# Key's product from seven products of halves, with D and value weights kept in DRAM, in an AdaLN layer with a scanned attention and a squared-ReLU mixer

## The chip, the cores and the metric

The kernel runs on one core of one Trainium2 chip. The metric is the device time of one execution in microseconds (us); lower is better. A core has TensorE (PE, the matrix multiplier, with its weight loads listed as PEld), VectorE (DVE), ScalarE (ACT), GpSimd (POOL) and SyncE (SP, which here only issues DMA transfers). Each executes its own instructions in order and waits on semaphores for the others.

## The reference

Inputs are `x` of shape (4, 2048, 512), float32, and weights. Everything is computed in float32.

```python
def layer(x):
    mod = (silu(c) @ wmod).reshape(4, 6, 1, 512)
    sa, ca, ga, sb, cb, gb = (mod[:, i] for i in range(6))
    ga, gb = (sign(g) * max(abs(g), 0.25) for g in (ga, gb))
    h = layernorm(x) * (1 + ca) + sa
    omega, zeta, F = softplus(h @ Wo.T + bo), sigmoid(h @ Wz.T + bz), h @ WB.T + bB
    # a linear recurrence over the 2048 positions, 2 x 64 states, gives xs
    x = x + ga * (xs @ C.T + h @ D.T)
    h = layernorm(x) * (1 + cb) + sb
    prev = shift_by_one_position(h)
    xr, xk = mu_r * h + (1 - mu_r) * prev, mu_k * h + (1 - mu_k) * prev
    k = square(relu(xk @ W_k))           # "Key"
    return x + gb * sigmoid(xr @ W_r) * (k @ W_v)
```

## The kernel before

The 2048 positions are cut into 8 blocks of W = 256, and each block into 4 units, one per batch row, so there are 32 units. Unit i has block s = i // 4 and row b = i % 4 (`at` in the loop). Each unit is worked on by a `Gates` object (its normalisation and the projection for the recurrence) and later by a `Finish` object. The final loop over `fin` runs one unit per turn. In turn i, for i from 4 on, the program order is:

- loads for later units (`load`), issued on SP;
- `key` of unit i (line 516): 16 products of 128x128 weights by 256 columns into two PSUM tiles of the pool tag "pm", which has two buffers. The product of 512 by 512 with 256 positions is cut into four output pieces and four contracted pieces. ACT then applies Relu (521) and Square (522);
- `norm_send(i + 9)`: statistics of a later unit, on ACT and POOL, and their row to DRAM;
- a pull `take(a)` of scan work;
- `attend` of unit i + 1: in two halves, the product with D (line 417, tag "px", three buffers), the product of the scan's states with C (446), then on DVE two additions to x (423, 460) and statistics (122, 123), with a pull `take(a2)` between the halves; then POOL (468, 469) and the normalisation `xn` on ACT (472);
- a pull `take(b_)`;
- `receptance` of unit i (530, tag "pm"), with a sigmoid on ACT (532);
- `mix` of unit i + 1: eight transposes of `xn` on TensorE (491), and from them eight pairs of one ACT (497) and one DVE instruction (500), the four of xk first, then the four of xr; POOL adds the first column (503) and, between the two fours, `shift` adds a row to a later x (410);
- `load_t`, `spread` on SP, and for units that still have a later block, `gates(i + 8)`: a projection (218), its scaling on DVE (224) and four ACT instructions (239);
- `value` of unit i: the product with W_v (545, tag "pm") in two halves, each multiplied and added on DVE (548, 549) and stored by SP (551), with a pull `take(c)` after the first half.

Instructions are issued to each engine in exactly this written order (`manual_schedule`); waits for data and for buffers are added by the framework.

The recurrence of one block (`scan`) is a list of steps, nearly all on DVE, each with a planned cost in us: two `soften` of 3.5, `chunk_step` of 0.7 once and 1.8 seven times, five `join` of 1.0, `fall_start` 0.8, five `fall` of 0.6 and eight `state_step` of 1.25, then `by_batch`, which copies on ACT and sends the states `y` through DMA. `take(budget)` issues steps until their planned costs have used the budget up. A block's scan is begun at the end of the turn with at = 3 (its ACT part, `soften_act`, at once), and pulled in the next three turns. In the turn with at = 2 the four budgets are shares of what is left.

`dg` holds D with the scale and gate of each row b folded in, `wvb` the value weights with the gate of each row folded in. Each is [128, 4, 4, 512] in SBUF, 1 MB per row b, and is built in the first four turns by `Turn` (`turn_d`, `turn_v`). Before, row b is read from place b throughout: `dg[:, u.b, k, :]` (417) and `wvb[:, u.b, k, at]` (545).

Of the kernel before, what the change touches and what calls it, by code (L numbers as in the profile page):

```python
# [21 lines left out]
P = 128  # L22
# [14 lines left out]
class Unit:  # L37


    def __init__(self, i):  # L40
        self.s, self.b = divmod(i, B)
        self.t0 = self.s * W
        self.tag = f"{self.s}_{self.b}"
# [3 lines left out]
def adaln_layer_kernel(ctx: ExitStack, tc: tile.TileContext, x, x_t, c_t, wmod, w_gate, w_b, b_gate, b_f, c_mat, d_mat,  # L47
# [342 lines left out]
    class Finish:  # L390


        def __init__(self, unit):
            self.u, self.tag = unit, f"c{unit.tag}"

        def room(self):
            self.x = p3.tile([P, NT, D], F32, tag="x", name=f"x_{self.u.tag}")

# [13 lines left out]
        def direct(self, n, room=(ps3, "px")):  # L412

            u = self.u
            pd = room[0].tile([P, D], F32, tag=room[1], name=f"pd_{self.tag}_{n}")
            for k in range(KC):
                nc.tensor.matmul(pd, self.h[:, k, ts(n, P)], dg[:, u.b, k, :], start=(k == 0), stop=(k == KC - 1))  # L417
            return pd

        def add_direct(self, n, pd):  # L420
# [4 lines left out]
        def products(self):  # L425

            self.pd = [self.direct(n) for n in range(NT)]
# [48 lines left out]
        def mix(self, between):  # L476
            xn, b = self.xn, self.u.b
            mixed = self.mixed = p1.tile([P, 2, KC, W], F32, tag="mixed", name=f"mixed_{self.tag}")
            edge = p2.tile([P, 2, KC], F32, tag="edge", name=f"edge_{self.tag}")
            if self.u.s == 0:  # L480
                nc.gpsimd.tensor_copy(edge, first_f[:, b])
            else:
                nc.gpsimd.tensor_tensor(
                    edge, prev_f[:, b], carry[:, b, :].unsqueeze(1).broadcast_to([P, 2, KC]), ALU.mult
                )
            pts = []
            for g in range(KC // 2):
                pt = ps2.tile([P, 2, W], F32, tag="pt", name=f"pt_{self.tag}_{g}")
                for j in range(2):
                    for n in range(NT):  # L490
                        nc.tensor.transpose(pt[:, j, ts(n, P)], xn[:, n, ts(2 * g + j, P)], ident)  # L491
                pts.append(pt)

            for i in (1, 0):
                for k in (0, 2, 1, 3):
                    pt, m = pts[k // 2][:, k % 2, :], mixed[:, i, k, :]
                    nc.scalar.activation(  # L497
                        m, pt, AF.Identity, bias=mod[:, SB, k, b : b + 1], scale=now_f[:, b, i, k : k + 1]
                    )
                    nc.vector.scalar_tensor_tensor(  # L500
                        m[:, 1:], pt[:, : W - 1], prev_f[:, b, i, k : k + 1], m[:, 1:], ALU.mult, ALU.add
                    )
                nc.gpsimd.tensor_tensor(mixed[:, i, :, 0], mixed[:, i, :, 0], edge[:, i, :], ALU.add)  # L503
                if i == 1:
                    between()
            for g, pt in enumerate(pts):
                nc.vector.tensor_copy(carry[:, b, 2 * g : 2 * g + 2], pt[:, :, W - 1])

        def key(self):
            mixed = self.mixed  # L510
            act = self.act = p1.tile([P, KC, W], F32, tag="act", name=f"act_{self.tag}")
            for e in range(KC // 2):
                pk = ps2.tile([P, 2, W], F32, tag="pm", name=f"pk_{self.tag}_{e}")
                for j in range(2):
                    for k in range(KC):
                        nc.tensor.matmul(  # L516
                            pk[:, j, :], wk[:, k, ts(2 * e + j, P)], mixed[:, 1, k, :],
                            start=(k == 0), stop=(k == KC - 1),
                        )
                a = act[:, 2 * e : 2 * e + 2, :]  # L520
                nc.scalar.activation(a, pk, AF.Relu)  # L521
                nc.scalar.activation(a, a, AF.Square)

        def receptance(self):
            mixed = self.mixed
# [9 lines left out]
        def value(self, between, parts=1):  # L535

            act, xt, u = self.act, self.x, self.u
            n_col = D // parts
            for n in range(NT):
                pv = ps2.tile([P, D], F32, tag="pm", name=f"pv_{self.tag}_{n}")  # L540
                r = self.r[n]
                for h in range(parts):
                    at = ts(h, n_col)
                    for k in range(KC):
                        nc.tensor.matmul(  # L545
                            pv[:, at], act[:, k, ts(n, P)], wvb[:, u.b, k, at], start=(k == 0), stop=(k == KC - 1)
                        )
                    nc.vector.tensor_mul(r[:, at], pv[:, at], r[:, at])  # L548
                    nc.vector.tensor_add(r[:, at], r[:, at], xt[:, n, at])
                    queue = nc.scalar if h else nc.sync  # L550
                    queue.dma_start(out[u.b, u.t0 + n * P : u.t0 + (n + 1) * P, at], r[:, at])
                if n == 0:
                    between()

    fin = [Finish(Unit(i)) for i in range(NB * B)]
    gts = [Gates(Unit(i)) for i in range(NB * B)]
# [297 lines left out]
    nc.scalar.copy(d0row, pr[:B, :])  # L854
    turn_d[0].turn()
    turn_d[0].keep()
    row = mod_rows(wm_sb, "sb", room=px)
    xt67 = wvb[:, 2].rearrange("p k d -> p (k d)").rearrange("p (i k w) -> p i k w", i=2, k=KC)
    for i in (6, 7):
# [11 lines left out]
    fin[0].products()  # L871
    turn_d[1].turn()
    turn_d[1].keep()
    turn_c[1].rows()
    gts[4].project()
    pcas = [scale_rows(b, pm) for b in range(2, B)]
# [40 lines left out]
    def gates(j):  # L917
        gts[j].project()
        gts[j].multiply()
        gts[j].deliver()  # L920
# [14 lines left out]
    for i, f in enumerate(fin):  # L935
        at = i % B
        ahead = fin[i + 1] if i + 1 < len(fin) else None
        if i < 4:
            if i == 3:
                take(100)  # L940
            fin[i + 2].load()
            gts[i + 10].load()
            f.key()
            if i < 2:
                rows(turn_d[i + 2], turn_c[i + 2])
            if i == 0:
                gts[6].project()
                gts[6].multiply()
                gts[6].deliver(share=True)
            else:  # L950
                norm_send(i + 9)
            if i == 3:
                gates(11)
            take(6)
            ahead.attend(lambda: take(2))
            turn(turn_v[i])
            if i == 0:
                gts[7].project()
                gts[7].multiply()
                gts[7].deliver(share=True)  # L960
                gts[8].norm_dve()
                gts[8].send()
                gts[8].spread()
                gts[9].norm_dve()
                gts[9].send()
            if i == 1:
                gates(9)
            if i:
                take(5)
            f.receptance()  # L970
            ahead.mix(fin[i + 2].shift)
            if i == 0:
                side += scan(1)
                take(0.1)
            gts[i + 9].load_t()
            gts[i + 9].spread()
            if i < 3:
                turn_v[i + 1].rows()
            f.value(lambda: take(3 if i == 0 else 4))
            if i < 2:  # L980
                turn(turn_d[i + 2], turn_c[i + 2])
                gates(8 if i == 0 else 10)
        else:
            if at == B - 1:
                take(100)
            if i + 2 < len(fin):
                fin[i + 2].load()
            if i + 10 < len(gts):
                gts[i + 10].load()
            f.key()  # L990
            if i + 9 < len(gts):
                norm_send(i + 9)
            if at == B - 2:
                left = sum(e[1] for e in side if e)
                a, a2, b_, c = 0.45 * left, 0.11 * left, 0.33 * left, 0.11 * left
            else:
                a, a2, b_, c = 5.5, 1.2, 4.0, 1.2
            take(a)
            if ahead:
                ahead.attend(lambda: take(a2))  # L1000
            take(b_)
            f.receptance()
            if ahead:
                ahead.mix(fin[i + 2].shift if i + 2 < len(fin) else lambda: None)
            if i + 9 < len(gts):
                gts[i + 9].load_t()
                gts[i + 9].spread()
            if i + 8 < len(gts):
                gates(i + 8)
            f.value(lambda: take(c), parts=1 if ahead else 2)  # L1010
        if at == B - 1 and i + 8 < len(gts):
            assert not side
            side += scan(i // B + 2)
            take(0.1)
# [43 lines left out]
```

## Time and profile before

| | before |
|---|---|
| median of 3 runs | 1167.98 us (1167.53 to 1168.3) |
| the profiled execution, own time | 1168.53 us |
| its span in the profile | 1166.8 us |
| granted TensorE clock, mean | 0.993 |
| PE busy | 1146.4 us, 98% |
| DVE busy | 704.1 us, 60% |
| ACT busy | 562.9 us, 48% |
| POOL busy | 160.7 us, 14% |
| moved by DMA | 102.29 MB, mean 88 GB/s |

The profile describes one execution. A row of a group gives the source line, the engine, the operation, output<-inputs, the shape and count, then busy time, mean nanoseconds of one, and the engine's idle time just before, with what ended it. A timeline row gives start and length in us, then the same names, and in brackets the idle time before. A row of a stretch (A:B) gives its length and the busy time with the count of instructions of PE, PEld, DVE, ACT and POOL in this order, then granted clock, DMA share and GB/s. Matmuls are pipelined, so the length of one record is longer than the distance to the next; the distance is what a stream costs.

### The profile page before, as it was taken

Reading aid. Unit: us, or ns where it says so; the run is one execution under the profiler, and the core shown is the slowest. Engines: PE = TensorE matmul, PEld = TensorE weight load, DVE = VectorE, ACT = ScalarE, POOL = GpSimd, SP = SyncE. Lnnn points to the kernel's source line nnn. Section 1 sums busy time; section 2 is a strip of 40 time slices with the busy share of each in tenths; the row PEclk is TensorE's granted clock in tenths of the full one; section 3 lists DMA queues with packets and bytes.
Section 4 is the critical chain, followed back from the end, with each engine's and each line's share of the span. In section 5 each row is a group of like instructions: output and inputs, shape, how many; then the busy total and the mean of one; then the engine's idle time right before and its main releaser. Section 6 shows DMA issues by size and latency. Waiting matters only on the chain.

```text
span 1166.8 us, 12040 instructions
## 1 busy us (share of the span) xinstructions
PE 1146.4 (98%) x3768; PEld 671.9 (58%) x3768; DVE 704.1 (60%) x1919; ACT 562.9 (48%) x1046; POOL 160.7 (14%) x290
## 2 busy tenths in 40 slices
PE   7998999999999999999999999999999999999998
PEld 3454666655655666556566655555666555555555
DVE  5696577548753677537763586537764497633332
ACT  1656777565334653546345644445454533333331
POOL 0132101111101111111111111101111111111100
PEclk9998999999999999999999999999999999999999
DMA  9744353232333322233234322342323111121101
GB/s 316 252 117 83 72 105 90 76 82 80 89 89 102 90 86 86 59 95 96 80 88 113 86 71 65 87 112 78 94 73 83 32 44 55 54 63 55 54 19 37
DMA packets 116801, 102.29 MB, mean 88 GB/s; under 512 B 14721, under 2 KB 87425, under 8 KB 116737
## 3 DMA queue, kind: packets, MB, share of 16 engines
q1 hardware_dynamic: 113728, 100.20, 30.8%
q0 software_dynamic: 320, 0.53, 0.3%
q10 hardware_dynamic: 2688, 0.79, 0.3%
q8 instruction: 30, 0.49, 0.2%
q14 instruction: 35, 0.28, 0.1%
HBM read 80.49 MB, written 16.81 MB: 83 GB/s over the span
## 4 chain that ended last, share of the span: by engine, by line
PE 96%; DVE 2%; ACT 1%; DMA 0%; issue 0%; POOL 0%; SPq 0%; DVEq 0%
PE pk_c L516 19%; PE pv_c L545 19%; PE pr_c L530 19%; PE pd_c L417 18%; PE pg L218 9%; PE pc_c L446 5%; PE pt_c L491 2%; PE turn_d L720 1%; PE turn_v L720 1%; PE rows_ca L633 1%; PE pd L118 0%; PE pca L118 0%; DMA wvb<-in_wmod_dram 0%; PE rows_sb L633 0%; PE rows_mean L633 0%; PE rows_gb L633 0%
## 5 line engine op out<-in xcount | busy, mean ns | idle before, releaser
L516 PE MATMUL pk_c<-mixed_c,wk 128*128 128x256 f32 x1024 | 229.4, 383 | 4.6 <-POOL mixed_c L503 4.6
L417 PE MATMUL pd_c<-dg,xt 128*128 128x512 f32 x512 | 231.7, 596 | 0.0
L545 PE MATMUL pv_c<-wvb,act_c 128*128 128x512 f32 (+1 forms) x528 | 225.5, 580 | 1.1 <-DVE r_c L548 1.1
L530 PE MATMUL pr_c<-wr,mixed_c 128*128 128x512 f32 x512 | 224.9, 592 | 0.0
L516 PEld LDWEIGHTS pk_c<-mixed_c,wk 128*128 128x128 f32 x1024 | 196.6, 192 | 44.5 <-issue 13.9
L500 DVE SCALAR_TENSOR_TENSOR mixed_c<-pt_c,prev_f,mixed_c 128x255 f32<-128x255 f32 x256 | 118.1, 482 | 131.4 <-ACT mixed_c L497 131.4
L472 ACT ACTIVATE xn_c<-x,nmr_c,rstd_c 128x512 f32<-128x512 f32 x64 | 48.6, 806 | 257.7 <-POOL nmr_c L469 257.7
L530 PEld LDWEIGHTS pr_c<-wr,mixed_c 128*128 128x128 f32 x512 | 97.1, 190 | 120.2 <-issue 119.6
L417 PEld LDWEIGHTS pd_c<-dg,xt 128*128 128x128 f32 x512 | 97.8, 191 | 111.0 <-issue 108.0
L545 PEld LDWEIGHTS pv_c<-wvb,act_c 128*128 128x128 f32 x528 | 99.3, 190 | 107.9 <-issue 102.6
L423 DVE SCALAR_TENSOR_TENSOR x<-pd_c,rs,x 128x512 f32<-128x512 f32 x64 | 47.7, 747 | 156.2 <-PE pd_c L417 156.2
L497 ACT ACTIVATE mixed_c<-pt_c,mod,now_f 128x256 f32<-128x256 f32 x256 | 130.4, 561 | 11.6 <-DVE mixed_c L500 5.3
L521 ACT ACTIVATE act_c<-pk_c 128x512 f32<-128x512 f32 x64 | 38.2, 598 | 187.9 <-PE pk_c L516 187.9
L218 PE MATMUL pg<-xt,wgb 128*128 128x256 f32 x448 | 103.0, 384 | 0.0
L548 DVE TENSOR_TENSOR r_c<-pv_c,r_c 128x512 f32<-128x512 f32 (+1 forms) x66 | 44.4, 672 | 76.6 <-PE pv_c L545 74.0
L218 PEld LDWEIGHTS pg<-xt,wgb 128*128 128x128 f32 x448 | 84.2, 193 | 10.7
L410 POOL TENSOR_TENSOR x<-x,d 128x1024 f32<-128x1024 f32 x31 | 73.0, 2355 | 0.8 <-ACT d L757 0.8
L446 PE MATMUL pc_c<-cg,y 128*128 128x512 f32 x128 | 65.1, 593 | 1.3 <-DMA y<-pre 1.3
L239 ACT ACTIVATE pre<-g,bias 64x256 f32<-64x256 f32 x64 | 46.9, 733 | 38.7 <-DVE g L224 32.3
L468 POOL TENSOR_TENSOR rstd_c<-rstd_c,neg_half 128x2 f32<-128x2 f32 x32 | 24.4, 762 | 298.1 <-DVE nmr_c L467 298.1
L532 ACT ACTIVATE r_c<-pr_c 128x512 f32<-128x512 f32 x64 | 37.0, 590 | 49.0 <-PE pr_c L530 48.9
L184 POOL TENSOR_SCALAR var<-var 128x2 f32<-128x2 f32 x26 | 5.1, 197 | 378.5 <-ACT xs L180 378.4
(189 smaller groups left out, 1108.0 us busy)
## 6 DMA issues: line engine op xcount, KB each, us to landing
xt<-in_x_t_dram SPq DMA_DIRECT2D x116, 256.0 KB, 5.3
x<-in_x_dram SPq DMA_DIRECT2D x32, 512.0 KB, 3.9
out_dram<-r_c SPq DMA_DIRECT2D x62, 256.0 KB, 2.1
xs<-in_x_dram SPq DMA_DIRECT2D x54, 256.0 KB, 4.2
wvb<-in_wmod_dram SPq DMA_DIRECT2D x5, 1024.0 KB, 10.2
y<-pre SPq DMA_DIRECT2D x64, 64.0 KB, 2.0
bc<-st SPq DMA_DIRECT2D x24, 128.0 KB, 4.8
wvb<-in_x_t_dram SPq DMA_DIRECT2D x8, 256.0 KB, 10.5
```

What stands on the lines that cost most here:

```text
L218: nc.tensor.matmul(self.pg[:, i, :], wgb[:, b, k, ts(i, P)], self.xt[:, k, :], start=(k == 0), stop=(k == KC - 1))
L239: nc.scalar.activation(there, here, AF.Identity, bias=bias[src, i, b : b + 1])
L410: nc.gpsimd.tensor_tensor(xt, xt, d0[:, self.u.b, :].unsqueeze(1).broadcast_to([P, NT, D]), ALU.add)
L417: nc.tensor.matmul(pd, self.h[:, k, ts(n, P)], dg[:, u.b, k, :], start=(k == 0), stop=(k == KC - 1))
L423: nc.vector.scalar_tensor_tensor(xt, pd, r, xt, ALU.mult, ALU.add)
L446: nc.tensor.matmul(pc, y_of[u.s][:, u.b, ts(n, P)], cg[:, u.b, :], start=(self.row is None), stop=True)
L472: nc.scalar.activation(self.xn[:, n, :], xt[:, n, :], AF.Identity, bias=nmr[:, n : n + 1], scale=rstd[:, n : n + 1])
L497: nc.scalar.activation(m, pt, AF.Identity, bias=mod[:, SB, k, b : b + 1], scale=now_f[:, b, i, k : k + 1])
L500: nc.vector.scalar_tensor_tensor(m[:, 1:], pt[:, : W - 1], prev_f[:, b, i, k : k + 1], m[:, 1:], ALU.mult, ALU.add)
L516: nc.tensor.matmul(pk[:, j, :], wk[:, k, ts(2 * e + j, P)], mixed[:, 1, k, :], start=(k == 0), stop=(k == KC - 1),)
L530: nc.tensor.matmul(pr, mixed[:, 0, k, ts(n, P)], wr[:, k, :], start=(k == 0), stop=(k == KC - 1))
L545: nc.tensor.matmul(pv[:, at], act[:, k, ts(n, P)], wvb[:, u.b, k, at], start=(k == 0), stop=(k == KC - 1))
```

## The change

From unit 4 on (`fast`, block s > 0), Key is computed by a scheme of seven products of halves (Winograd's form of Strassen's). The weight W_k, with 512 contracted by 512 output columns, and the mixed input, with 512 by 256 positions, are each cut into two by two quarters. Seven products of quarters, of 256 by 256 by 128, take the place of the eight that a product by quarters needs.

- `make_key_weights` forms four sums of weight quarters once, with four DVE instructions, in the turn i = 2. They lie in the room of `dg` for row 2.
- `key_sums` forms four sums of input quarters for each unit, on DVE, in `mix` after the four instructions of xk and before `shift`. They lie in the room of `dg` for row 3, in two halves used in turn.
- `key_fast` has four groups of products (two, two, two and one), each group in a tile of tag "pm", 28 matmuls of 128x128 by 128 columns. One copy and seven additions take the products from PSUM to `act`: the additions are on DVE, the copy is on DVE for row b = 0 and on ACT for the others. Relu and Square follow on ACT, now from `act`.
- With two rows of `dg` used for the sums, D of a fast unit is read from place i % 2, and so are its value weights. All four rows of both are stored once to DRAM (`keep_in_dram`, eight DMAs on SP), and for units 6 to 31 both are fetched from there (`fetch`, 1 MB each, on SP): D for unit i + 3 after `attend` of turn i, value weights for unit i + 2 at the end of turn i.
- The budgets of the pulls change: from 5.5, 1.2, 4.0, 1.2 to 3.0, 0, 7.0, 1.2 (at = 0) and 3.6, 1.2, 5.5, 1.2 (at = 1), and for at = 2 the shares from 0.45, 0.11, 0.33, 0.11 to 0.33, 0.11, 0.45, 0.11.

```diff
+            self.fast = unit.s > 0
+            self.at = unit.i % 2 if self.fast else unit.b
...
-                nc.tensor.matmul(pd, self.h[:, k, ts(n, P)], dg[:, u.b, k, :], start=(k == 0), stop=(k == KC - 1))
+                nc.tensor.matmul(pd, self.h[:, k, ts(n, P)], dg[:, self.at, k, :], start=(k == 0), stop=(k == KC - 1))
...
                 if i == 1:
+                    if self.fast:
+                        self.key_sums()
                     between()
...
+        def key_sums(self):
+            (b00, b01), (b10, b11) = self.quarters = [
+                [self.mixed[:, 1, 2 * k : 2 * k + 2, ts(t, P)] for t in range(2)] for k in range(2)
+            ]
+            half = dg[:, 3].rearrange("p k d -> p (k d)")[:, ts(self.u.i % 2, 2 * D)]
+            t = self.sums = half.rearrange("p (i k w) -> p i k w", i=4, k=2)
+            nc.vector.tensor_sub(t[:, 0], b01, b00)
+            nc.vector.tensor_sub(t[:, 1], b11, t[:, 0])
+            nc.vector.tensor_sub(t[:, 2], b11, b01)
+            nc.vector.tensor_sub(t[:, 3], b10, t[:, 1])
+
+        def key_fast(self):
+            (b00, b01), (b10, b11) = self.quarters
+            t, s = self.sums, key_weights
+            act = self.act = p1.tile([P, KC, W], F32, tag="act", name=f"act_{self.tag}")
+            (c00, c01), (c10, c11) = [[act[:, 2 * o : 2 * o + 2, ts(h, P)] for h in range(2)] for o in range(2)]
+
+            def products(*pairs):
+                pk = ps2.tile([P, 2, 2, P], F32, tag="pm", name=f"pk_{self.tag}")
+                for n, (left, right) in enumerate(pairs):
+                    for j in range(2):
+                        for k in range(2):
+                            nc.tensor.matmul(
+                                pk[:, n, j, :], left[:, k, ts(j, P)], right[:, k, :], start=(k == 0), stop=(k == 1)
+                            )
+                return pk[:, 0], pk[:, 1]
+
+            add = nc.vector.tensor_add
+            x1, x2 = products((wk[:, 0:2, : D // 2], b00), (wk[:, 2:4, : D // 2], b10))
+            copy = nc.scalar.copy if self.u.b else nc.vector.tensor_copy
+            copy(c01, x1)
+            add(c00, c01, x2)
+            x6, x5 = products((s[:, 1], t[:, 1]), (s[:, 0], t[:, 0]))
+            add(c10, c01, x6)
+            add(c01, c10, x5)
+            x7, x3 = products((s[:, 2], t[:, 2]), (s[:, 3], b11))
+            add(c11, c01, x7)
+            add(c10, c10, x7)
+            add(c01, c01, x3)
+            x4, _ = products((wk[:, 2:4, D // 2 :], t[:, 3]))
+            add(c10, c10, x4)
+            for e in range(KC // 2):
+                a = self.act[:, 2 * e : 2 * e + 2, :]
+                nc.scalar.activation(a, a, AF.Relu)
+                self.squares(e)
...
-                            pv[:, at], act[:, k, ts(n, P)], wvb[:, u.b, k, at], start=(k == 0), stop=(k == KC - 1)
+                            pv[:, at], act[:, k, ts(n, P)], wvb[:, self.at, k, at], start=(k == 0), stop=(k == KC - 1)
...
+    def make_key_weights():
...
+        nc.vector.tensor_add(s[:, 0], a10, a11)
+        nc.vector.tensor_sub(s[:, 1], s[:, 0], a00)
+        nc.vector.tensor_sub(s[:, 2], a00, a10)
+        nc.vector.tensor_sub(s[:, 3], a01, s[:, 1])
...
+    def keep_in_dram(name, b):
+        src = dg if name == "dg" else wvb
+        nc.sync.dma_start(kept[name][b], src[:, b].rearrange("p k d -> p (k d)"))
+
+    def fetch(name, i):
+
+        if 6 <= i < len(fin):
+            dst = dg if name == "dg" else wvb
+            nc.sync.dma_start(dst[:, i % 2].rearrange("p k d -> p (k d)"), kept[name][i % B])
...
+            if i == 2:
+                make_key_weights()
             ahead.attend(lambda: take(2))
             turn(turn_v[i])
+            keep_in_dram("wv", i)
+            if i == 3:
+                fetch("dg", i + 3)
...
-            f.key()
+            f.key_fast()
...
-                a, a2, b_, c = 0.45 * left, 0.11 * left, 0.33 * left, 0.11 * left
+                a, a2, b_, c = 0.33 * left, 0.11 * left, 0.45 * left, 0.11 * left
             else:
-                a, a2, b_, c = 5.5, 1.2, 4.0, 1.2
+                a, a2, b_, c = (3.6, 1.2, 5.5, 1.2) if at else (3.0, 0.0, 7.0, 1.2)
             take(a)
             if ahead:
                 ahead.attend(lambda: take(a2))
+            fetch("dg", i + 3)
             take(b_)
...
             f.value(lambda: take(c), parts=1 if ahead else 2)
+            fetch("wv", i + 2)
```

More of the change, by code (lines that the diff above doesn't have):

```diff
@@ L40, in __init__ @@
     def __init__(self, i):
+        self.i = i
         self.s, self.b = divmod(i, B)
@@ L507, in mix, with squares @@
                 nc.vector.tensor_copy(carry[:, b, 2 * g : 2 * g + 2], pt[:, :, W - 1])
+        def squares(self, e):
+            a = self.act[:, 2 * e : 2 * e + 2, :]
+            nc.scalar.activation(a, a, AF.Square)
         def key(self):
@@ L519, in key @@
                         )
-                a = act[:, 2 * e : 2 * e + 2, :]
-                nc.scalar.activation(a, pk, AF.Relu)
-                nc.scalar.activation(a, a, AF.Square)
+                nc.scalar.activation(act[:, 2 * e : 2 * e + 2, :], pk, AF.Relu)
+                self.squares(e)
[9 more added lines that the diff above has]
+            nc.vector.tensor_sub(t[:, 3], b10, t[:, 1])
@@ new lines, in key_fast @@
+        def key_fast(self):
[27 more added lines that the diff above has]
+            for e in range(KC // 2):
+                a = self.act[:, 2 * e : 2 * e + 2, :]
+                nc.scalar.activation(a, a, AF.Relu)
+                self.squares(e)
@@ L553, in value @@
                     between()
+    key_weights = dg[:, 2].rearrange("p k d -> p (k d)").rearrange("p (i k o) -> p i k o", i=4, k=2)
+    def make_key_weights():
+        s = key_weights
+        (a00, a01), (a10, a11) = [
+            [wk[:, 2 * k : 2 * k + 2, ts(o, D // 2)] for k in range(2)] for o in range(2)
+        ]
+        nc.vector.tensor_add(s[:, 0], a10, a11)
+        nc.vector.tensor_sub(s[:, 1], s[:, 0], a00)
+        nc.vector.tensor_sub(s[:, 2], a00, a10)
+        nc.vector.tensor_sub(s[:, 3], a01, s[:, 1])
+    kept = {
+        name: [dram.tile([P, KC * D], F32, tag=f"{name}{b}", name=f"{name}{b}") for b in range(B)]
+        for name in ("dg", "wv")
+    }
+    def keep_in_dram(name, b):
[5 more added lines that the diff above has]
+            nc.sync.dma_start(dst[:, i % 2].rearrange("p k d -> p (k d)"), kept[name][i % B])
     fin = [Finish(Unit(i)) for i in range(NB * B)]
@@ L856, in adaln_layer_kernel @@
     turn_d[0].keep()
+    keep_in_dram("dg", 0)
     row = mod_rows(wm_sb, "sb", room=px)
@@ L873, in adaln_layer_kernel @@
     turn_d[1].keep()
+    keep_in_dram("dg", 1)
     turn_c[1].rows()
@@ L981, in adaln_layer_kernel @@
                 turn(turn_d[i + 2], turn_c[i + 2])
+                keep_in_dram("dg", i + 2)
                 gates(8 if i == 0 else 10)
```

## The prediction

> **What bounds the kernel now.** I read the page's busy shares and its chain first, then TensorE's timeline over one unit, then the busy time of every engine unit by unit, then who waits for whom.
>
> ```profile
> PE 1146.4 (98%) x3768; PEld 671.9 (58%) x3768; DVE 704.1 (60%) x1919; ACT 562.9 (48%) x1046; POOL 160.7 (14%) x290
> ...
> PE 96%; DVE 2%; ACT 1%; DMA 0%; issue 0%; POOL 0%; SPq 0%; DVEq 0%
> ```
>
> The end is set by TensorE's own stream. Nothing else is worth shortening, and anything that makes TensorE wait is paid in full. One unit on TensorE, without a gap:
>
> ```profile
> 627.65 7.07 PE L516 MATMUL pk_c<-mixed_c,wk 128*128 128x256 f32 x32
> 634.56 3.60 PE L417 MATMUL pd_c<-dg,xt 128*128 128x512 f32 x8
> ...
> 643.14 7.03 PE L530 MATMUL pr_c<-wr,mixed_c 128*128 128x512 f32 x16
> 650.01 1.04 PE L491 MATMUL pt_c<-ident,xn_c 128*128 128x128 f32 x8
> ...
> 654.34 7.03 PE L545 MATMUL pv_c<-wvb,act_c 128*128 128x512 f32 x16
> 661.20 7.07 PE L516 MATMUL pk_c<-mixed_c,wk 128*128 128x256 f32 x32
> ```
>
> From start to start Key takes 6.91 us: 32 records, 215.9 ns each. The unit takes 33.55 us. The four units of a block (at = 0 to 3), with DVE in the third column of busy times:
>
> ```profile
> 526.99:560.55 33.56, 33.56 (x110) 19.83 (x109) 27.71 (x64) 19.62 (x37) 5.06 (x8) 1.00 0.28 83
> 560.55:594.10 33.55, 33.55 (x110) 19.82 (x108) 23.76 (x79) 14.61 (x28) 4.60 (x8) 1.00 0.31 82
> 594.10:627.65 33.55, 33.55 (x109) 19.83 (x108) 19.42 (x61) 16.38 (x32) 4.72 (x8) 1.00 0.31 83
> 627.65:661.20 33.55, 33.55 (x109) 19.83 (x108) 12.06 (x25) 16.63 (x31) 4.58 (x8) 1.00 0.39 98
> ```
>
> DVE has 12 us of the unit's own work and 7 to 16 us of scan in three of the four. It executes in order, so where its spare time lies decides. The granted clock is 1.00.
>
> **TensorE's part.** A fast unit (4 to 31, so 28 of them) has 28 products of 128x128 by 128 columns. Each fp32 product shows as two records, so 32 records become 56. Their pace is the first unknown. From below: half of 215.9, 108 ns. From above: a load not overlapped at all, 192 ns. The trace has the very form in L209, 128x128 f32 by 128 columns, and a load-bound run in L799 (4 columns):
>
> ```profile
> 35.69 0.36 PE L209 MATMUL pb<-cg,ones 128*128 128x128 f32 x1
> ...
> 35.69 0.69 PE L209 MATMUL pb<-cg,ones 128*128 128x128 f32 x4
> ...
> 33.88 1.86 PEld L799 LDWEIGHTS pbias<-mod,wraw 128*128 128x128 f32 x16 [0.35 <-DVE mod L795]
> ```
>
> These L209 lines are the timeline up to 35.8 us and up to 36.15: three more records end 0.33 us later, 110 ns each. L799's 16 loads take (1.86 - 0.19) / 15 = 111 ns each. I take 111.5: 56 x 111.5 = 6.24 us, a saving of 0.665 us a unit, 18.6 us over 28.
>
> [...] L209's rows are fp32 and of the right width, and the one-pass transposes agree (L491: (1.04 - 0.273) / 7 = 110 ns), so the rows decide. Only four two-pass records in a row have been seen, so a few ns stay open; each costs 1.57 us over 28 units before waits.
>
> **DVE's part.** Added per unit: four sums of quarters in the mix, and one copy and seven adds in Key (from unit b = 1 on, ACT makes the copy). All are 128x256 f32:
>
> ```profile
> L549 DVE TENSOR_TENSOR r_c<-r_c,x 128x256 f32<-128x256 f32 x4 | 1.7, 425 | 0.1
> L548 DVE TENSOR_TENSOR r_c<-pv_c,r_c 128x256 f32<-128x256 f32 x4 | 1.7, 424 | 18.3 <-PE pv_c L545 18.3
> ```
>
> PSUM or SBUF makes no difference. Dependent ones start 0.46 apart (L548 to L549 at 1156.08); independent ones overlap by 0.09 (L299 to L300: 0.36 long, 0.27 apart), so 0.34. Sums: 0.46 + 3 x 0.34 = 1.5 us. Key: about 2.8. Bounds for each of the twelve: 0.3 us if they overlap better (192 elements start 0.27 apart), 0.6 if each exposes a semaphore's delay. They are purely added, so none can gain.
>
> Now the queues, with t = 0 at Key's first record and about 0.2 us from a matmul's slot to its reader (L545 to L548). Product groups occupy TensorE at 0, 1.78, 3.57 and 5.35, to 6.24. DVE first ends the previous unit's value (two of 0.69, from 0.2 to 1.6), then the copy and first add (to 2.8), frees the third group's bank before 3.57, does two adds (3.8 to 4.45, before 5.35), three (5.56 to 6.7) and the last (to 7.0). So Key's own handshakes fit, with 0.7 us to spare each. But DVE is now tied to Key until 7.0, where before it ran 5 to 7 us of scan. That scan moves behind.
>
> - at = 3, no scan: attend and mix are at their old places; the sums lie in idle time (6.1 us before the mix now). Full saving.
> - at = 0: pull 3.0 is one soften (3.7, to 10.7; its ACT part ended at 3.3 before, 4.5 now). Attend's second half waits for TensorE at 14.2 and ends at 16.85. Pull 7.0 is a soften, the first chunk and two more (7.9 with a wait for three ACT copies), to 24.8, so the mix starts 2 us late: four at 0.46, sums 1.5, four at 0.46, carry, gate product, value's first product end at 31.5, its add 32.2, a chunk at 34.0. The next Key starts at 32.9; its second group needs the bank of value's second product, free at 34.75, against 34.67: 0.1 us lost.
> - at = 1: the same path ends with nothing lost.
> - at = 2: 13.0 of planned scan is left (8.75 before, since the first two units pull less). The share of 0.33 pulls five falls and two state steps, 3.5 + 2.3 us, so attend starts at 12.85 (before: DVE waited 4.4 us for TensorE here). Then first half 2.4, two states 2.3, second half 2.65: 20.2. POOL 1.2, ACT's two xn 1.5: 22.9 to 23.0. TensorE finishes receptance at 21.7 and wants xn for the transposes: 1.36 us lost.
> - Units 24 to 27 have no gates, so TensorE has 3.45 us less from transposes to Key, and the same DVE work: 0.4 + 1.1 + 1.4 + 0.9 + 0.2 = 4.0 on top of the 1.36.
> - Last unit: receptance waits for the third group's adds, 0.5.
>
> Lost: 6 x 1.36 + 5 x 0.1 + 4.0 + 0.5 = 13.2 us. The same bookkeeping with before's order gives no wait and 33.56 us a unit.
>
> **What I cost at nothing.** SP gets eight stores and 52 fetches of 1 MB. Each issue is about 0.4 us in a queue that already sits waiting for DVE's results (396.6 us at L551 in SP's waits). The value weights' fetch waits for value's last matmul, but stands behind the output, which is ready 1.4 us later; D's fetch waits for attend at 13.9, with the statistics' row and the next transposed loads behind it, which are wanted a unit later. Each fetch is issued over one unit before its use; 1 MB took 10.2 us. Traffic rises from 83 to about 146 GB/s; the first slice of the page moved 316. The row of y (eight DMAs, 8.8 us from the first ACT copy to landing) is issued ahead of the value fetch and lands at about 8.5, wanted at 9.7. That is the thinnest cover: without it, up to 1 us in each of 6 blocks. POOL's edge (0.2 us) ends before the fourth mix instruction does, so the sums do not wait for it. Key's weight sums (four of 0.69, once) lie in the 3.03 us that DVE idles at 199 to 202. ACT keeps its two Relu and two Square; a Relu from PSUM (0.60) and a Square from SBUF (0.63) last alike, and value wants them 17 us later.
>
> **Sum.** -18.6 + 13.2 = -5.4, against the profiled execution: span 1166.8, own time 1168.5, 0.55 above the median. 1168.0 - 5.5 = 1162.5.
>
> **The rivals.**
> 1. As worked, 0.46: 1162.5, its own range 1158 to 1166.
> 2. Nearly the full saving, 0.14: the scan's real order leaves DVE room. All twelve at 0.34 or less and scan 5% shorter give -12; -18.6 with no wait: 1149 to 1156. For it: at = 3 is idle. Against: the 20.2 at at = 2 is a chain of measured durations.
> 3. Slower, 0.27: DVE's in-order lag. Each added instruction takes 0.6 as it waits for its predecessor's result, and sums 2.2. The mix then ends 0.7 us later in every scan unit and value's banks free late, in the gateless units every time. The same bookkeeping gives +7, and +11 with the scan 3% longer: 1175 to 1179. It decides from about 0.5 us of extra sums per unit. For: the at = 0 unit is full already. Against: the 424 ns rows.
> 4. Slower, 0.08: the two-pass pace does not hold 56 long. Break-even at 115 ns; 120 gives +6, 134 gives +27: 1174 to 1195.
> 5. Late fetches or y, 0.05: 1 us in 28 units gives 1190. This is also the case in which the change doesn't do what it says, its fetched weights not coming beside other work. Against: DMA share 0.31.
>
> About 0.2% (2.3 us) is what a measurement of this kernel can tell. Faster: 0.40 of case 1 and case 2, 0.54. Same: 0.06, 0.05 of case 3 and 0.02 of the rest, 0.13. Slower: 0.33. Range 1153 to 1180: it leaves out the best of case 2 and the worst of 4 and 5.
>
> **What would show it.** Right: 56 records in 6.2 us at Key; the transposes waiting on ACT's xn by about 1.4 us in every third unit of a block; units of 32.9, 33.0, 34.3, 32.9. Wrong: Key's groups waiting on DVE inside Key (case 3), loads spaced over 115 ns (4), TensorE waiting on a DMA into dg, wvb or y (5), no wait at the transposes (2).

## The result, and the profile after

| | before | after |
|---|---|---|
| median of 4 runs each, one chip | 1167.76 us (1166.87 to 1168.3) | 1194.98 us (1194.51 to 1199.47) |
| ratio, 95% interval | | 1.0242 [1.0217, 1.0268] |
| span of the profiled execution | 1166.8 us | 1192.7 us |
| PE busy | 1146.4 us, 98% | 1140.3 us, 96% |
| DVE busy | 704.1 us | 867.1 us |
| moved by DMA | 102.29 MB | 165.32 MB |

The change is slower, by 27.2 us in the medians and 25.9 us in the spans. The forecast was 1162.5 us, with a range up to 1180, so it missed in sign and size. The chain that ended last, from the page of the kernel after:

```profile
PE 65%; DVE 26%; ACT 5%; issue 3%; DMA 1%; POOL 0%; DVEq 0%; SPq 0%; POOLq 0%
```

Before, TensorE was 96% of the chain. Now 26% of it runs over DVE: TensorE's stream has holes, and DVE's order fills them. The products themselves did what was forecast. TensorE's timeline at a Key that waits for nothing (start, length, engine, line, output<-inputs):

```profile
327.16 1.95 PE L562 MATMUL pk_c<-mixed_c,wk 128*128 128x128 f32 x16
328.94 2.84 PE L562 MATMUL pk_c<-dg 128*128 128x128 f32 x24
331.62 1.06 PE L562 MATMUL pk_c<-mixed_c,dg 128*128 128x128 f32 x8
332.51 1.06 PE L562 MATMUL pk_c<-dg,wk 128*128 128x128 f32 x8
333.41 3.60 PE L422 MATMUL pd_c<-dg,xt 128*128 128x512 f32 x8
```

56 records take 6.25 us from start to start (333.41 - 327.16), 111.6 ns each, where Key took 6.91. But the four units of a block, at = 0 to 3 (length, then busy time of PE, PEld, DVE, ACT and POOL, then clock, DMA share and GB/s), do not get shorter:

```profile
531.60:565.10 33.50, 33.03 (x134) 19.81 (x132) 28.30 (x61) 20.52 (x37) 4.82 (x8) 1.00 0.72 146
565.10:599.30 34.20, 33.26 (x133) 20.17 (x134) 30.21 (x81) 15.61 (x32) 5.09 (x8) 1.00 0.69 142
599.30:633.20 33.90, 33.31 (x134) 19.92 (x133) 29.62 (x97) 14.31 (x29) 4.85 (x8) 1.00 0.68 144
633.20:667.40 34.20, 33.16 (x133) 20.07 (x132) 18.09 (x37) 17.32 (x35) 4.63 (x8) 1.00 0.67 158
```

They were 33.55 each; forecast were 32.9, 33.0, 34.3 and 32.9. What TensorE waits for (us in total, times, longest):

```profile
PE pk_c L562 <- DVE r_c L610: 22.6, 18, 3.3
PE pk_c L562 <- DVE act_c L571: 5.4, 5, 1.2
...
PE pt_c L496 <- ACT xn_c L477: 3.7, 12, 0.4
```

Key waits 28.0 us for DVE. L610 is the product by which the *previous* unit's value frees a bank of the tag "pm". None of this was in the list of before. So DVE reaches value's arithmetic late. What makes it late stands in its groups by form (busy us, mean ns of one, idle before):

```profile
L546 DVE TENSOR_TENSOR dg<-mixed_c 128x256 f32<-128x256 f32 x28 | 67.3, 2403 | 0.0
...
L580 DVE TENSOR_TENSOR act_c<-act_c,pk_c 128x256 f32<-128x256 f32 x28 | 11.6, 416 | 0.1
```

The added instructions last 0.41 to 0.43 us each, but for one: the first sum of a unit lasts 2.40 us in the mean. Its two inputs are ready and it shows no idle time before it. The timeline of POOL and DVE around one of them shows what runs beside it:

```profile
285.63 0.20 POOL L508 TENSOR_TENSOR mixed_c<-mixed_c,edge_c 128x4 f32<-128x4 f32 x1 [7.92 <-ACT mixed_c L502]
285.78 2.35 POOL L415 TENSOR_TENSOR x<-x,d 128x1024 f32<-128x1024 f32 x1
...
285.93 2.48 DVE L546 TENSOR_TENSOR dg<-mixed_c 128x256 f32<-128x256 f32 x1
288.44 0.42 DVE L547 TENSOR_TENSOR dg<-mixed_c,dg 128x256 f32<-128x256 f32 x1
```

POOL's `shift` (L415, 2.35 us), issued right behind the edge (L508), starts 0.15 us before the sum, and the sum ends 0.28 us after it: 285.78 + 2.35 = 288.13, against 288.41. The sum looks as if it stood still while `shift` ran. The wait is inside a busy record (2.48 us, with no idle time before it), so no list of waits names it. Only the mean of the group, 2403 ns, betrays it. In the same unit TensorE's next Key then looks so:

```profile
292.98 2.02 PE L562 MATMUL pk_c<-mixed_c,wk 128*128 128x128 f32 x16 [0.47 <-DVE r_c L610]
295.94 2.94 PE L562 MATMUL pk_c<-dg 128*128 128x128 f32 x24 [0.94 <-DVE r_c L610]
```

The theory to be tested (L, the lock): a DVE instruction with two inputs from SBUF does not proceed while `shift` runs on GpSimd, so the first sum waits for the whole of it. The rivals: the seven products with twelve added DVE instructions are too much for DVE wherever the sums stand (D); the 63 MB of added DMA traffic (fetches and stores) disturb the others (F).

### The profile page after: what moved, and what is told of

The parts are those of the page before. It is cut to its first block, busy times and chain, and to the rows that moved or that the text cites. A ratio compares the mean times of both kernels' runs of the same rounds, so it can differ in the third digit from the quotient of the medians.

```text
span 1192.7 us, 13937 instructions
## 1 busy us (share of the span) xinstructions
PE 1140.3 (96%) x4440; PEld 680.1 (57%) x4440; DVE 867.1 (73%) x2238; ACT 567.4 (48%) x1067; POOL 163.4 (14%) x290
## 2 busy tenths in 40 slices
DMA packets 125449, 165.32 MB, mean 139 GB/s; under 512 B 15680, under 2 KB 88384, under 8 KB 117696
## 4 chain that ended last, share of the span: by engine, by line
PE 65%; DVE 26%; ACT 5%; issue 3%; DMA 1%; POOL 0%; DVEq 0%; SPq 0%; POOLq 0%
PE pd_c L422 14%; PE pk_c L562 13%; PE pr_c L592 12%; PE pv_c L607 9%; PE pg L219 6%; PE pc_c L451 4%; DVE dg L546 4%; DVE mixed_c L505 3%; PE pk_c L527 2%; ACT mixed_c L502 2%; DVE stats_c L123 1%; DVE x L465 1%; DVE uv L363 1%; DVE r_c L610 1%; PE pt_c L496 1%
## 5 line engine op out<-in xcount | busy, mean ns | idle before, releaser
L502 ACT ACTIVATE mixed_c<-pt_c,mod,now_f 128x256 f32<-128x256 f32 x256 | 130.4, 561 | 111.5 <-DVE mixed_c L505 107.9
L562 PE MATMUL pk_c<-dg 128*128 128x128 f32 x672 | 83.9, 281 | 10.6 <-DVE act_c L571 5.4
L562 PEld LDWEIGHTS pk_c<-dg 128*128 128x128 f32 x672 | 80.1, 197 | 12.8 <-DVE act_c L571 6.4
L583 ACT ACTIVATE act_c<-act_c 128x512 f32<-128x512 f32 x56 | 34.8, 622 | 109.2 <-DVE act_c L578 109.2
L562 PEld LDWEIGHTS pk_c<-mixed_c,wk 128*128 128x128 f32 x448 | 55.7, 199 | 34.8 <-issue 34.3
L562 PE MATMUL pk_c<-mixed_c,wk 128*128 128x128 f32 x448 | 58.2, 286 | 17.4 <-DVE r_c L610 17.4
L415 POOL TENSOR_TENSOR x<-x,d 128x1024 f32<-128x1024 f32 x31 | 72.8, 2349 | 0.0
L546 DVE TENSOR_TENSOR dg<-mixed_c 128x256 f32<-128x256 f32 x28 | 67.3, 2403 | 0.0
```

What stands on the lines that cost most here:

```text
L415: nc.gpsimd.tensor_tensor(xt, xt, d0[:, self.u.b, :].unsqueeze(1).broadcast_to([P, NT, D]), ALU.add)
L502: nc.scalar.activation(m, pt, AF.Identity, bias=mod[:, SB, k, b : b + 1], scale=now_f[:, b, i, k : k + 1])
L546: nc.vector.tensor_sub(t[:, 0], b01, b00)
L562: nc.tensor.matmul(pk[:, n, j, :], left[:, k, ts(j, P)], right[:, k, :], start=(k == 0), stop=(k == 1))
```

## Experiments

All comparisons are with the kernel before, run on the same chip, where its median is 1166.28 us for the first four experiments and 1167.05 us for the other four. "Units" are distances from one Key's first record to the next.

### The change without `shift`

The fast turns leave out `shift`, so the row that it adds to a later x is missing from the output. The last of the first four turns keeps its own.

```diff
-                ahead.mix(fin[i + 2].shift if i + 2 < len(fin) else lambda: None)
+                ahead.mix(lambda: None)
```

> The changed kernel, but the POOL instruction `shift` behind the first edge of each fast mix is left out (so the row d0 is not added to x there). Lock theory (the first of the four key sums, with two SBUF inputs, stands still while POOL's 2.35 us `shift` runs): the first sum falls from 2.4 us to 0.42 us in all 28 units, TensorE's waits on value's banks at Key's first groups fall from 28 us in total to a few, and the time is about 1163 us (the prediction's working without the stall, 1160 to 1168). Rival A (fetch traffic slows the sums or SP): the first sum stays at 2.4 us, the time stays within 3 us of 1195. Rival B (DVE simply has too many instructions): the first sum gets short, but the time stays above 1180.

Measured: 1163.06 us (1159.28 to 1163.97), ratio 0.9967 [0.9957, 0.9977]. The first sum's group, and TensorE's waits:

```profile
L546 DVE TENSOR_TENSOR dg<-mixed_c 128x256 f32<-128x256 f32 x28 | 13.7, 488 | 0.0
```
```profile
PE pk_c L562 <- DVE r_c L610: 4.9, 5, 1.9
```

27 first sums last 0.42 us and the one that still has its `shift` 2.48; their mean is the 488 ns. Key's waits for value fall from 22.6 to 4.9 us. The units of a block are 32.90, 32.90, 33.90 and 32.90. So with `shift` gone the change gains, and DVE's added work as such does not make it slow: D falls. This kernel also has 59 us less of POOL work (104.0 against 163.4), so it does not yet show that the *meeting* of the two instructions is the cause.

### The sums moved, `shift` kept

The four sums are issued between the halves of value, after its first product and addition, when `shift` is over.

```diff
-                    if self.fast:
-                        self.key_sums()
...
-            f.value(lambda: take(c), parts=1 if ahead else 2)
+            f.value(lambda: (ahead.key_sums() if ahead else None, take(c)), parts=1 if ahead else 2)
```

> The changed kernel with the four key sums issued later on DVE, between the two halves of value instead of between the two fours of the mix; nothing is left out. `shift` then runs beside mix instructions that read PSUM and one SBUF tensor. Lock theory: every sum 0.42 us, time about 1164 us (1160 to 1169; the bookkeeping gives 3.4 us below before). Rival A (traffic): sums elsewhere long again, time near 1195. Rival B (amount of DVE work, which is the same here): time stays above 1180.

Measured: 1162.37 us (1160.68 to 1163.4), ratio 0.9963 [0.9948, 0.9978]. Key waits 3.2 us for value, in two. The timeline of POOL and DVE:

```profile
282.93 2.36 POOL L415 TENSOR_TENSOR x<-x,d 128x1024 f32<-128x1024 f32 x1
...
287.60 0.42 DVE L544 TENSOR_TENSOR dg<-mixed_c 128x256 f32<-128x256 f32 x1
```
Every instruction of the change is there, `shift` included. Only the order differs, and 32.6 us of the 1194.98 are gone (in ratios to before, 0.9963 against 1.0242). It is the meeting, not the work.

### The fetches alone

The kernel before with D and value weights kept in DRAM and fetched as in the change; Key and the budgets as before.

> The kernel before with only the storage part of the change: D and value weights of the later blocks stored to DRAM and fetched for each unit, Key as before, budgets as before. Lock theory: the fetches are not the cause, 1168 us within 2 us. Rival A (traffic or SP's queue): a large part of the 27 us is here, 1180 or more.

Measured: 1166.17 us, ratio 1.0001 [0.9993, 1.001], units 33.55. The fetches cost nothing: F falls.

### One subtraction in the kernel before, from SBUF and from PSUM

If L holds, it needs no Strassen. The kernel before gets one 128x256 subtraction in front of `shift`, in units 4 to 31, into a buffer that is free there. In the first form both inputs lie in SBUF, in the second the first input is the PSUM tile of the transposes.

```diff
                 if i == 1:
+                    if self.u.s:
+                        probe = xn[:, 0, : 2 * P].rearrange("p (k w) -> p k w", k=2)
+                        nc.vector.tensor_sub(probe, mixed[:, 1, 2:4, P:], mixed[:, 1, 0:2, P:])
                     between()
```
```diff
-                        nc.vector.tensor_sub(probe, mixed[:, 1, 2:4, P:], mixed[:, 1, 0:2, P:])
+                        nc.vector.tensor_sub(probe, pts[1][:, :, P:], mixed[:, 1, 0:2, P:])
```

> The kernel before plus one DVE subtraction per unit from block 1 on, 128x256, both inputs in SBUF, at the place of the first key sum; its result is not used. Lock theory: it lasts 2.4 to 2.5 us instead of 0.42 us although there is no fetch and no fast Key here, and the kernel gets slower: with 2.48 us inserted the bookkeeping gives 13 us more, 1178 to 1182, lost in units with at = 0 and in the units without gates. Rival A (fetch traffic makes the sum long): 0.42 us and 1168.

> As the kernel before with one DVE subtraction per unit at the place of the first key sum, but with its first input read from PSUM (the transposed tile) and the second from SBUF; same size, place and wait, result not used. Lock theory (two SBUF inputs are what meets `shift`): 0.42 us each, time 1166 to 1168 as before. Rival C (any DVE instruction issued there is slow, by the wait on POOL's edge or on the queue): 2.3 us each and about 1179 as with two SBUF inputs.

Measured: from SBUF 1178.59 us (1178.13 to 1179.07), ratio 1.0103 [1.0088, 1.0118]; from PSUM 1167.48 us (1166.36 to 1168.17), ratio 0.9998 [0.9989, 1.0006]. The group and the timeline, from SBUF:

```profile
L507 DVE TENSOR_TENSOR xn_c<-mixed_c 128x256 f32<-128x256 f32 x28 | 64.2, 2291 | 1.0
```
```profile
555.27 2.34 POOL L410 TENSOR_TENSOR x<-x,d 128x1024 f32<-128x1024 f32 x1
...
555.55 2.35 DVE L507 TENSOR_TENSOR xn_c<-mixed_c 128x256 f32<-128x256 f32 x1
```

and from PSUM:

```profile
L507 DVE TENSOR_TENSOR xn_c<-pt_c,mixed_c 128x256 f32<-128x256 f32 x28 | 11.6, 415 | 0.0
```
```profile
551.00 2.35 POOL L410 TENSOR_TENSOR x<-x,d 128x1024 f32<-128x1024 f32 x1
...
551.15 0.41 DVE L507 TENSOR_TENSOR xn_c<-pt_c,mixed_c 128x256 f32<-128x256 f32 x1
```

One operation, one size, one place, beside the same 2.35 us of `shift`: 2.29 us or 0.415. Only the first input, and with it the memory that it lies in, separates them. For `shift`, L is shown, and a single such instruction per unit is worth 1% of this kernel. It also accounts for why `mix` itself, in the trace of before, runs beside `shift` at its usual 0.48 us: its instructions (L500, 482 ns in the mean of all 256) take one tensor from PSUM and one from SBUF.

### `shift` in two halves

If the sum waits for one whole GpSimd instruction, two shorter ones might let it in between.

```diff
-            nc.gpsimd.tensor_tensor(xt, xt, d0[:, self.u.b, :].unsqueeze(1).broadcast_to([P, NT, D]), ALU.add)
+            for n in range(NT):
+                nc.gpsimd.tensor_tensor(xt[:, n, :], xt[:, n, :], d0[:, self.u.b, :], ALU.add)
```

> The changed kernel with `shift` as two POOL instructions of 128x512 in place of one of 128x1024. Lock theory, held for one POOL instruction at a time: if DVE gets its turn between the two, the first sum lasts about 1.2 to 1.5 us and the bookkeeping gives 5 us above before, about 1172; if the second half takes the port again at once, the sum stays at 2.4 us and the time at about 1194. A theory in which the two only share bandwidth expects no change in the sum, 2.4 us.

Measured: 1190.69 us (1189.88 to 1191.47), ratio 1.0202 [1.0187, 1.0217]. The timeline:

```profile
287.61 2.67 POOL L416 TENSOR_TENSOR x<-x,d 128x512 f32<-128x512 f32 x2
...
287.76 1.40 DVE L547 TENSOR_TENSOR dg<-mixed_c 128x256 f32<-128x256 f32 x1
289.19 1.37 DVE L548 TENSOR_TENSOR dg<-mixed_c,dg 128x256 f32<-128x256 f32 x1
```

The first sum gets in after the first half (1.40 us), and then the second sum waits for the second half (1.37 us). The turns alternate, one instruction each. The four sums take 3.47 us from the first start to the last end, against 3.60 with one `shift` and 1.54 with none beside them. The two shorter instructions divide the wait here and hardly shorten it. The expectation missed this: it put the time near 1172 if DVE got its turn, and DVE got it, but only for one instruction.

### `shift` at the end of the mix

The order the other way round: the sums stay and `shift` is issued after the second edge of fast units.

```diff
                     if self.fast:
                         self.key_sums()
-                    between()
+                    else:
+                        between()
...
+            if self.fast:
+                between()
```

> The changed kernel with the key sums in their place and POOL's `shift` issued behind the second edge instead of the first; nothing is left out. Lock theory: the sums are all 0.42 us; `shift` now meets carry, the gate product and value's first product (one SBUF input each, not held up) and then value's addition of two SBUF inputs or a scan chunk, which is held up by up to 0.9 us in units with gates and 1.5 us in those without: 1163 to 1172. Rival B (amount of DVE work): above 1180.

Measured: 1167.96 us (1166.95 to 1168.97), ratio 1.0008 [0.9999, 1.0016]. All sums last 0.42 us. The group of value's addition and the timeline of POOL and DVE:

```profile
L614 DVE TENSOR_TENSOR r_c<-r_c,x 128x512 f32<-128x512 f32 x62 | 56.6, 913 | 2.1
```
```profile
288.23 2.36 POOL L415 TENSOR_TENSOR x<-x,d 128x1024 f32<-128x1024 f32 x1
...
289.17 0.68 DVE L613 TENSOR_TENSOR r_c<-pv_c,r_c 128x512 f32<-128x512 f32 x1
289.88 1.25 DVE L614 TENSOR_TENSOR r_c<-r_c,x 128x512 f32<-128x512 f32 x1
```

`shift` now meets another DVE instruction that reads two tensors from SBUF. L613 takes one input from PSUM and passes at 0.68; L614 takes both from SBUF and lasts 1.25 here, 913 ns in the mean, where it had 692 before. 62 additions at 0.22 us more are 13.7 us of DVE, and this kernel stands 5.6 us above the one that moves the sums (1167.96 against 1162.37); that all of the 5.6 is the lock on L614 is argued, not shown.

### The sums moved and the pulls set anew

The sums between the halves of value, as above. There the transposes of the turn at = 2 still wait for `xn`. In this kernel the shares of that turn's four pulls are changed so that `attend` comes earlier.

```diff
-                a, a2, b_, c = 0.33 * left, 0.11 * left, 0.45 * left, 0.11 * left
+                a, a2, b_, c = 0.2 * left, 0.11 * left, 0.5 * left, 0.19 * left
```

> The version with the key sums between the halves of value, and in the turn with at = 2 the shares of scan changed from 0.33, 0.11, 0.45, 0.11 to 0.20, 0.11, 0.50, 0.19, so that less scan stands ahead of attend. If the wait of the transposes for xn in these turns comes from that pull, as the prediction worked out, it vanishes: units of 32.9 instead of 33.9 at at = 2, about 6 us less than with the sums moved alone: 1155 to 1157. If the wait has another cause, 1162 as without it.

Measured: 1157.36 us (1156.16 to 1157.69), ratio 0.9914 [0.9898, 0.9931], faster than both kernels: 9.7 us under before in the same comparison, where the sums moved alone gave 3.9, and 37.6 under the median of after. That is 0.4 us above the expected range. Units are 32.90, 33.25, 32.90 and 32.90. No wait for `xn` is left; of Key's waits for value 4.0 us remain, in four.

## Why the prediction was wrong, point by point

**TensorE's part was right.** 56 records at 111.5 ns were forecast and 111.6 measured, from four records of L209 in a row and a stretch of weight loads. The pace of the fourth rival was not needed.

**The fetches and the row of y were right.** They were costed at nothing. The DMA share rose to 0.7, with the forecast 146 GB/s, and the kernel with the fetches alone stands at 1.0001.

**DVE's price of the sums is the step that failed.** The text has "Sums: 0.46 + 3 x 0.34 = 1.5 us". They take 3.6 us from the first start to the last end (285.93 to 289.54), in 27 of the 28 units; the last unit's mix has no `shift`, and its first sum lasted 415 ns. The 0.42 itself was right wherever `shift` did not run beside it (418 to 425 ns in the mean for the second to fourth sums). The failure sits in one sentence of "What I cost at nothing": "POOL's edge (0.2 us) ends before the fourth mix instruction does, so the sums do not wait for it." I looked at POOL only for a result that the sums need. The instruction issued directly behind that edge, `shift`, shares no data with them, and I passed over it. "PSUM or SBUF makes no difference" was read from rows with POOL idle (425 and 424 ns), and is false with `shift` beside (2291 and 415 ns).

The trace of before holds one such meeting that I did not see. One of the 56 scan products L362, both of whose inputs lie in SBUF, starts 0.1 us behind a `shift` and lasts 2.38 us, where the median of its group is 0.29:

```profile
85.85 2.33 POOL L410 TENSOR_TENSOR x<-x,d 128x1024 f32<-128x1024 f32 x1 [0.79 <-ACT d L757]
85.95 2.38 DVE L362 TENSOR_TENSOR uv<-f,pre 128x128 f32<-128x128 f32 x1
```

All other DVE instructions that start beside a `shift` there are L500, with one input in PSUM.

The runs agree with one another: 2.40 us behind `shift` against 0.42; 2.29 against 0.415 by moving one input to PSUM; and, with `shift` in two halves, the second half lasts 1.45 us beside the sums and the first 1.27. In all of them `shift` is the GpSimd instruction; none tries another. With the excess measured here, 2.48 - 0.42 = 2.06 us, the sums of the forecast would have been 1.5 + 2.06 = 3.56 us. The forecast's bookkeeping, given the right length, comes out right at least in the kernel before with one subtraction: with 2.48 us put in at that place it gave 13 us more, ahead of the run, and 12.3 were measured (1178.59 against 1166.28).

**Where 25.9 us came from.** TensorE's saving is 18.6. Against it stand 28.0 us of waits in Key and 3.7 at the transposes, 35 of them; at each about 0.17 us of the last record's modelled end has nothing beside it (a 512-column record shows 0.60 where the distance is 0.43), some 6 us; 0.08 to 0.10 us more for each of the 23 waits in Key, whose first 40 records take 4.54 us behind a wait and 4.46 without one, some 2 us; and 5.0 us of a lower clock (last section). The estimate is -18.6 + 31.7 + 6 + 2 + 5.0 = 26.1.

By place, most of it lies in the last units, which have no gates: from Key to Key the 20 units from the first fast one on take 679.7 us against 671.1 before, the seven after them 227.5 against 210.7, 16.8 us of the 25.9. In the last three of these no scan is left either, and the delay of the sums is paid in full: unit 29 takes 31.55 us, and 29.49 without `shift`, 2.06 less. The forecast had given all gateless units together 5.4 us of waits.

**The third rival had the right side and the wrong cause.** It put the loss on DVE's in-order lag, named the place (mix late, value's banks late, gateless units every time) and the point from which it decides, 0.5 us of extra sums per unit. The extra was 2.06 us. But its mechanism, 0.6 us for each added instruction as it waits for its predecessor's result, does not occur: they last 0.41 to 0.43, and where no `shift` is beside them the second sum starts 0.45 us behind the first, which it reads.

**With the lock taken out, the first case holds.** It gave 1162.5, with its own range from 1158 to 1166. Without `shift` the kernel ran at 1163.06, with the sums moved at 1162.37. That these lie so close to 1162.5 is in part luck: on that chip the kernel before stands at 1166.28, so they gain 3.2 and 3.9 us where 5.5 were forecast. Without `shift`, 2.0 us of what is missing lie in the turn before the first fast Key, whose mix keeps its `shift` (37.34 us to the next Key, against 35.30 with the fetches alone). Units of 32.90 came as forecast, and the seven last units lose 5.2 us to waits, forecast 5.4. The wait for `xn` at at = 2, forecast at 1.36 us (its own terms, 22.9 to 23.0 against 21.7, give 1.2 to 1.3), is 1.0 (33.90 - 32.90). The kernel after shows it in the same size: 3.7 us in 12 waits, against 3.6 without `shift`.

**Key's own handshakes** were forecast to fit, with 0.7 us to spare each. They fit once DVE is on time: the 5.4 us that wait for L571 in after are not in the lists of the kernels without the lock.

## What to carry to other kernels

Before an instruction is put on DVE, list where each of its inputs lies and what GpSimd executes in that window, whether or not they share data: with two SBUF inputs it took 2.06 us more here behind a `shift` of 2.35 us (2.48 against 0.42). Look at the mean of a group by form against the same form elsewhere (2403 ns against 416): this lock showed as busy time and in no list of waits. The remedies that worked here: issue it when GpSimd is idle (32.6 us), or take one input from PSUM (11.1 us for the one subtraction); cutting the GpSimd instruction left 3.47 of the sums' 3.60 us, and moving it to where another two-input instruction stands put 0.22 us on each of 62 additions.

## What the runs showed of the hardware that I had not expected

**The turns of the lock alternate.** With `shift` in two instructions in a row DVE gets exactly one of its own in between, and the next one waits again (1.40 and 1.37 us; 1362 and 1338 ns in the mean of all 28 units, of which 27 have a `shift` there).

**A lower clock follows some of TensorE's waits, and not others.** In units 25 to 30 of after, TensorE waits 1.9 to 3.3 us ahead of each Key. Its timeline at three of these Keys:

```profile
972.04 3.19 PE L562 MATMUL pk_c<-mixed_c,wk 128*128 128x128 f32 x16 [3.32 <-DVE r_c L610]
```
```profile
1039.15 2.02 PE L562 MATMUL pk_c<-mixed_c,wk 128*128 128x128 f32 x16 [2.40 <-DVE r_c L610]
```
```profile
1070.70 2.88 PE L562 MATMUL pk_c<-mixed_c,wk 128*128 128x128 f32 x16 [1.87 <-DVE r_c L610]
```

After the first and the third (and again at 1135.42) the granted clock is 0.66 over the next 5 us, and Key's first 40 records take 6.25, 6.17 and 6.16 us; after the longer wait of 2.40 us it stays at 1.00, and they take 4.54. The three together cost 5.0 us. The profile of before has no such place from 120 us to its last product. Without `shift` there is one, behind a wait of 1.88 us at the first fast Key (0.66 over the 5 us from 258.85, and 6.17 us for the first 40 records).

The traces show more of where it falls. In after the clock is 0.50 for 3.41 us each time, from 972.67, 1071.66 and 1136.51, and these starts lie 98.99 and 64.85 us apart, 29 and 19 times 3.413 us. Borders at this distance, drawn through the three starts, are an estimate of mine. On that grid, the two waits of 1.87 us with a fall behind them lie whole in the interval that ends where the clock falls, while the wait of 2.40 us is cut by a border into 0.77 and 1.63 us. But one wait of 1.88 us, ahead of the Key at 1005.32, begins 0.04 us behind a border, lies whole in its interval too, and had no fall behind it (1.00 over the next 5 us). So the grid does not settle which waits have a fall behind them.

This is read from the traces; that the waits cause the lower clock is not tried by a run of its own. If they do, a wait of 1.87 us on TensorE cost 1.87 + 1.6 us at these two Keys, nearly twice its length.
